# Moving the sum of two GRU cells from TensorE to VectorE for two column groups of a four-layer graph network

## The chip, the cores and the metric

The program runs on one core of one Trainium2 chip. The metric is device time of one execution in microseconds (us), taken as the median of several runs. The core has five engines that work at the same time, each through its own queue in order: TensorE (PE, matrix products into the accumulator memory PSUM), VectorE (DVE, element-wise work), ScalarE (ACT, activation functions and scaled copies), GpSimd (POOL) and SyncE (SP, which here starts transfers). They wait for each other through semaphores.

## The reference, cut to what matters

Four graph layers follow each other on 3327 nodes with 64 features. Each normalises the state, computes an update from the adjacency matrix and adds it to the state `X`. The change is in the third layer. It runs two GRU cells on the same hidden state `h` and adds both outputs, scaled row by row with the diagonal of the adjacency matrix:

```python
def gru_cell(x, h, w_ih, w_hh, b_ih, b_hh):
    gi = x @ w_ih.T + b_ih
    gh = h @ w_hh.T + b_hh
    ir, iz, inn = jnp.split(gi, 3, axis=1)
    hr, hz, hn = jnp.split(gh, 3, axis=1)
    r = jax.nn.sigmoid(ir + hr)
    z = jax.nn.sigmoid(iz + hz)
    n = jnp.tanh(inn + r * hn)
    return (1.0 - z) * n + z * h
...
    edge_output = gru_cell(node_support, h, w_ih_e, w_hh_e, b_ih_e, b_hh_e)
    edge_support = gat(h, A_node, A_edge, W_gat, a_gat)
    node_output = gru_cell(edge_support, h, w_ih_n, w_hh_n, b_ih_n, b_hh_n)
    return d_edge[:, None] * edge_output + d_node[:, None] * node_output
```

Both adjacency arguments are the same matrix, so both diagonals are the same. With the output of a cell written as n + z (h - n), the update of a node is its diagonal entry times four terms: z0 (h - n0) + n0 + z1 (h - n1) + n1, where 0 is the first (edge) cell and 1 the second (node) cell.

## The kernel before, in words

The 3327 nodes are padded to 26 tiles of 128. In this layer the data lie feature-major: a tile such as `hP` has 128 partitions (64 features of the first 13 node tiles, and 64 of the last 13) and 1664 columns (13 tiles of 128 nodes). The columns are worked in four groups, `COLS`: group 0 has four tiles (512 columns), groups 1, 2 and 3 have three each (384 columns). A step `u` is one cell on one group: steps 0 to 3 are the first cell on groups 0 to 3, steps 4 to 7 the second cell on groups 0 to 3.

Each step has these pieces, named as in the code:

- `products(u)` (lines 1968 to 1980): eight TensorE products into four PSUM banks. Two slots of two banks serve the even steps, two others the odd ones, so step u writes the banks of step u - 2.
- `sigmoids(u)` (line 1988): ScalarE makes the gates r and z. The buffer of z is used again three steps later.
- `before_tanh(u)` (lines 1995, 1996): VectorE makes the argument of the tanh from two PSUM banks and the gate r.
- `tanh(u)` (line 1999): ScalarE, in place, gives n. For the first cell n lies in `xh[0][0]` (the trace calls it xh), for the second in `deg`.
- `state(u)` (lines 2001 to 2015): VectorE makes o = z (h - n) with a subtraction (2008) and a product (2011). For the first cell o lies in `oP` (the trace calls it own), for the second in `hP` itself.

The queues are in program order. In turn u of the loop the order is `products(u)`, `sigmoids(u)`, `tanh(u - 1)`, then `before_tanh(u)`, copies for the second cell (`take2`, ScalarE), `state(u - 1)`. After the loop comes the way back to node-major layout:

- `turn_back(k)` (lines 2020 to 2032): for each 128-column block of group k, TensorE multiplies each term with the identity and adds the products up in PSUM, which transposes the block and sums its terms at once. A group with one term takes a plain transpose (2029). `turn_back(0)` and `turn_back(1)` write to one PSUM slot (banks 4 and 5), `turn_back(2)` and `turn_back(3)` to another (banks 6 and 7).
- `scale(k)` (lines 2038 to 2047): ScalarE multiplies with the diagonal, one 64-column piece per instruction; for group 3 VectorE does it in one (2042).
- `use(k)` (line 2051): VectorE adds to `X`.

The terms differ by group in the kernel before. In groups 0 and 1 TensorE sums four terms (own, xh, hP, deg). In group 2 VectorE adds xh to own (2013) and TensorE sums three. In group 3 VectorE sums all four (2013, 2010, 2015) and TensorE transposes one.

`turn_back(0)` stands in the last turn of the loop, after `tanh(6)` and ahead of `before_tanh(7)`. After the loop the order is: `tanh(7)`, `scale(0)`, `turn_back(1)`, `scale(1)`, `turn_back(2)`, `state(7)`, `use(0)`, `turn_back(3)`, `use(1)`, `scale(2)`, `scale(3)`, `use(2)`, `use(3)`. Waits are kept per slot, not per bank. So in the built program the first product of `turn_back(1)` waits for the last instruction of `scale(0)`, and `scale(2)` waits for the last transpose of `turn_back(3)`. The fourth layer begins on VectorE with the row sums of `X` (line 449), after the last `use`.

Of the kernel before, what the change touches and what calls it, by code (L numbers as in the profile page):

```python
# [49 lines left out]
def tile_gnn4(ctx: ExitStack, tc: tile.TileContext, x, adjT, att0, b0, w1, bias1, w_gat, a_gat,  # L50
# [1778 lines left out]
    def plain_gat(masks, zo, deg, first, wg, gru, H, parts, banks, last_x, finish, close):  # L1829
# [8 lines left out]
        C = len(COLS)  # L1838
        with ExitStack() as st:
            def bank(k):  # L1840
                return banks[k]

            def of(k, at=0):
                t, n = COLS[k]
                return slice(at + t * P, at + (t + n) * P)
# [39 lines left out]
            hP = pers.tile([P, HP], F32, name="hP")  # L1885

            xh = [[pers.tile([P, HP], F32, name=f"xh{g}{o}") for o in range(2)] for g in range(2)]
            oP = H.rearrange("p k o d -> p (k o d)")
# [3 lines left out]
            for _ in range(1):  # L1892
# [108 lines left out]
                def state(u):  # L2001


                    g, k = steps[u]
                    cs = of(k)
                    nn, z = nns[u], gates[u][1]
                    o, h = (oP, hP)[g][:, cs], hP[:, cs]
                    V.tensor_sub(o, h, nn)
                    if g == 1 and k == C - 1:
                        V.tensor_add(nn, nn, oP[:, cs])  # L2010
                    V.tensor_mul(o, o, z)
                    if g == 0 and k > 1:
                        V.tensor_add(o, o, nn)
                    if g == 1 and k == C - 1:
                        V.tensor_add(oP[:, cs], o, nn)
# [3 lines left out]

                def turn_back(k):  # L2020

                    terms = [oP] if k == C - 1 else [oP, hP, deg] if k > 1 else [oP, xh[0][0], hP, deg]
                    t0, n = COLS[k]
                    pt = turned[k] = bank(4 + k)
                    for t in range(n):
                        cs = slice((t0 + t) * P, (t0 + t + 1) * P)
                        for i, src in enumerate(terms):
                            if len(terms) == 1:
                                PE.transpose(pt[:, t * P:(t + 1) * P], src[:, cs], ident)
                            else:  # L2030
                                PE.matmul(pt[:, t * P:(t + 1) * P], src[:, cs], ident, start=i == 0,  # L2031
                                          stop=i == len(terms) - 1)
# [28 lines left out]
                for u in range(K):  # L2061
                    products(u)
                    sigmoids(u)
                    if u:
                        tanh(u - 1)
                    if u == K - 1:
                        turn_back(0)
                    before_tanh(u)
                    if u < C:
                        take2(u)  # L2070
                    if u:
                        state(u - 1)
                tanh(K - 1)
                scale(0)
                turn_back(1)
                scale(1)
                turn_back(2)
                state(K - 1)
                use(0)
                turn_back(3)  # L2080
# [108 lines left out]
```

## Time and profile before

| what | us |
|---|---|
| median of 3 runs (lowest, highest) | 721.95 (721.23, 726.72) |
| the profiled execution, whole | 726.15 |
| its span, first to last instruction | 724.4 |
| TensorE busy in the span | 639.9 (88%) |
| VectorE busy | 532.1 (73%) |
| ScalarE busy | 542.3 (75%) |
| first product of step 0 to last `use` | 430.39 to 465.74 |

The page of the profile gives busy time by engine, then the chain of work that ended last, followed back from the last instruction, with shares of the span. The timeline lists instructions by start and length in us, with the engine, the line of the kernel, output and inputs; a bracket at the end is the time that the engine was idle before and what released it. A product of two float32 operands shows as two TensorE instructions, so "x32" are 16 products. The table of stretches gives, for each, the busy time of the engines (with the number of instructions in brackets), and PEclk, the clock that TensorE was granted, as a share of full speed. All times count from the start of the span.

### The profile page before, as it was taken

Reading aid. Unit: us, or ns where it says so; the run is one execution under the profiler, and the core shown is the slowest. Engines: PE = TensorE matmul, PEld = TensorE weight load, DVE = VectorE, ACT = ScalarE, POOL = GpSimd, SP = SyncE. Lnnn points to the kernel's source line nnn. Section 1 sums busy time; section 2 is a strip of 40 time slices with the busy share of each in tenths; the row PEclk is TensorE's granted clock in tenths of the full one; section 3 lists DMA queues with packets and bytes.
Section 4 is the critical chain, followed back from the end, with each engine's and each line's share of the span. In section 5 each row is a group of like instructions: output and inputs, shape, how many; then the busy total and the mean of one; then the engine's idle time right before and its main releaser. Section 6 shows DMA issues by size and latency. Waiting matters only on the chain.

```text
span 724.4 us, 12112 instructions
## 1 busy us (share of the span) xinstructions
PE 639.9 (88%) x4291; PEld 262.8 (36%) x4291; DVE 532.1 (73%) x980; ACT 542.3 (75%) x720; POOL 433.4 (60%) x327
## 2 busy tenths in 40 slices
PE   0799999989999889989998999449999999999970
PEld 0522233333333333435445653442223433334320
DVE  6867778767777799999755429697767777777755
ACT  2778888878888785687881578368888889888853
POOL 2699999979999500305740000038887888888840
PEclk9999999999999999999999999869999999999995
DMA  3998888888888725489960000202234444443001
GB/s 64 315 288 262 267 267 261 277 254 260 282 252 274 254 81 199 140 292 328 404 243 1 2 1 1 94 18 76 91 94 135 118 119 139 117 118 117 24 2 51
DMA packets 61638, 119.25 MB, mean 165 GB/s; under 512 B 9568, under 2 KB 34048, under 8 KB 61568
## 3 DMA queue, kind: packets, MB, share of 16 engines
q1 hardware_dynamic: 57216, 118.38, 50.8%
q10 hardware_dynamic: 4352, 0.02, 0.3%
q8 instruction: 35, 0.57, 0.3%
q14 instruction: 35, 0.29, 0.1%
HBM read 115.64 MB, written 0.88 MB: 161 GB/s over the span
## 4 chain that ended last, share of the span: by engine, by line
PE 65%; DVE 13%; issue 6%; POOL 5%; DMA 4%; ACT 3%; SPq 2%; ACTq 1%; POOLq 0%; DVEq 0%
PE slot L653 18%; PE slot L661 10%; PE slot L632 9%; PE slot L633 8%; PE slot L1552 6%; PE slot L1859 5%; POOL sig L621 5%; PE slot L1566 4%; DMA adj<-in 3%; DVE same L1447 2%; PE slot L1975 2%; PE slot L2031 1%; DVE mask L1535 1%; ACT sig L618 1%; PE slot L1980 1%
## 5 line engine op out<-in xcount | busy, mean ns | idle before, releaser
L643 DVE SCALAR_TENSOR_TENSOR sig<-slot,sig 128x768 f32<-128x768 f32 (+2 forms) x209 | 212.8, 1018 | 112.9 <-POOL sig L621 108.0
L638 ACT ACTIVATE slot<-slot 128x768 f32<-128x768 f32 (+1 forms) x208 | 177.2, 852 | 59.6 <-PE slot L633 59.5
L621 POOL TENSOR_TENSOR sig<-adj,sig 128x768 f32<-128x768 f32 (+1 forms) x104 | 201.3, 1960 | 17.3 <-ACT sig L618 11.4
L618 ACT ACTIVATE sig<-leftB,right 128x768 f32<-128x768 f32 (+1 forms) x208 | 203.1, 976 | 0.1
L621 POOL TENSOR_TENSOR sig<-mask,sig 128x768 f32<-128x768 fp8e4 (+2 forms) x105 | 173.4, 1664 | 40.0 <-ACT sig L618 39.1
L653 PE MATMUL slot<-sig,Xr 128*64 128x384 f32 (+1 forms) x832 | 171.3, 530 | 7.0 <-DVE sig L643 6.9
L632 PE MATMUL slot<-XC,XT 128*128 128x384 f16 (+1 forms) x416 | 142.4, 342 | 2.6 <-ACT sum L671 1.7
L633 PE MATMUL slot<-XF,XE 73*128 73x384 f16 (+1 forms) x416 | 141.6, 340 | 0.0
L661 PE MATMUL slot<-sig,X 128*32 128x384 f32 (+1 forms) x832 | 95.7, 532 | 0.0
L1558 ACT ACTIVATE w<-slot,ebias 128x832 bf16<-128x832 f32 x76 | 69.1, 951 | 25.2 <-PE slot L1552 24.8
L653 PEld LDWEIGHTS slot<-sig,Xr 128*64 128x64 f32 x832 | 50.2, 136 | 88.4 <-issue 63.7
L632 PEld LDWEIGHTS <-XT 128*128 128x128 f16 x416 | 40.7, 98 | 95.3 <-issue 68.8
L1552 PE MATMUL slot<-mask,rest 128*128 128x416 fp8e4 x208 | 54.0, 341 | 5.2 <-ACT adj L1558 2.8
L1552 PE MATMUL slot<-mask,after 128*128 128x416 fp8e4 x208 | 53.4, 339 | 1.1 <-DVE deg L1576 1.1
L633 PEld LDWEIGHTS <-XE 73*128 73x128 f16 x416 | 40.8, 98 | 28.0 <-issue 3.6
L1447 DVE TENSOR_SCALAR_CACHE_REDUCE same<-late 128x832 fp8e4<-128x832 f32 x48 | 48.4, 1009 | 0.0
L219 POOL TENSOR_TENSOR mask<-mask,offdiag 128x128 fp8e4<-128x128 fp8e4 x26 | 17.5, 682 | 43.9 <-PE slot L1552 43.8
L436 POOL MEMSET X<- 128x832 f32 x2 | 1.6, 791 | 69.0 <-ACT xh L1966 69.0
L1859 PE MATMUL slot<-mask,own 128*64 128x384 fp8e4 (+1 forms) x416 | 39.8, 346 | 2.2 <-DVE deg L1576 2.2
L661 PEld LDWEIGHTS slot<-sig,X 128*32 128x32 f32 x832 | 16.5, 108 | 69.1 <-issue 66.7
L542 PE MATMUL pt<-ident_h,Xp 128*64 128x128 f16 x32 | 2.6, 314 | 37.6 <-ACT Xp L481 37.6
L1566 PE MATMUL slot<-w,h 128*64 128x416 bf16 x304 | 34.0, 345 | 0.0
(337 smaller groups left out, 699.4 us busy)
## 6 DMA issues: line engine op xcount, KB each, us to landing
adj<-in SPq DMA_DIRECT2D x78, 384.0 KB, 4.7
late<-in SPq DMA_DIRECT2D x48, 416.0 KB, 3.2
adj<-in SPq DMA_DIRECT2D x17, 832.0 KB, 7.2
adj<-in SPq DMA_DIRECT2D x27, 512.0 KB, 4.9
ahead<-in SPq DMA_DIRECT2D x14, 832.0 KB, 8.0
ahead<-in SPq DMA_DIRECT2D x16, 416.0 KB, 5.6
own<-in SPq DMA_DIRECT2D x16, 416.0 KB, 5.3
own<-in SPq DMA_DIRECT2D x8, 832.0 KB, 6.6
```

The source lines that it names most:

```text
L618: A.activation(sig, leftB[c], AF.Sigmoid, bias=right[:, b:b + 1])
L621: G.tensor_tensor(sig[:, os], adj[:, os], sig[:, os], op=OP.mult)
L632: PE.matmul(L[:, o, :c[1] * P], XT[:, rows], XC[c][:, o, :], start=True, stop=False)
L633: PE.matmul(L[:, o, :c[1] * P], XE[:KE, rows], XF[c][:, o, :], start=False, stop=True)
L638: A.activation(L, L, AF.Arctan, scale=PA / SX ** 2)
L643: V.scalar_tensor_tensor(sig[:, os], slot[:, os, :tiles[k][0][1] * P], PC, sig[:, os], op0=OP.add, op1=OP.mult)
L653: PE.matmul(acc[c][o * D:(o + 1) * D, 0, :n], Xr[:, b, :], sigs[k][:, o, :], start=b == 0, stop=b == T - 1)
L661: PE.matmul(acc[c][q:q + 32, 1, :n], X0[:, b - 1 + i, :], w[:, o, :], start=b == 1, stop=b == T - 1, tile_position=(0, q))
L1552: PE.matmul(cnt[o][:, h, :BK], w, cols(k, o, h), start=w is after and steps[k][1] == T - 1, stop=True, skip_group_check=True)
L1558: A.activation(ws[k][:, o, :, :], cnt[o][:, :, :BK], AF.Exp, scale=-LN2, bias=ebias)
L1566: PE.matmul(acc[c][o * D:(o + 1) * D, h, :BK], parts[i][:, b, :], w[:, o, h, :], start=b == T - 1 and i == 0, stop=b == 0 and i == 1)
L1859: PE.matmul(acc[k][o * D:(o + 1) * D, :], w, mask[:, of(k, o * HP)], start=n == 0 and i == 0, stop=n == T - 1 and i == 1)
```

## The change

VectorE adds n0 to own for every group of the first cell, not only for groups 2 and 3. For the second cell it adds own to `deg` in groups 0 and 1 as it did in group 3. TensorE then sums two terms in groups 0 and 1 (hP and deg), still three in group 2, and transposes one in group 3.

```diff
@@ state(u)
                     V.tensor_sub(o, h, nn)
-                    if g == 1 and k == C - 1:
+                    if g == 1 and k != 2:
                         V.tensor_add(nn, nn, oP[:, cs])
                     V.tensor_mul(o, o, z)
-                    if g == 0 and k > 1:
+                    if g == 0:
                         V.tensor_add(o, o, nn)
                     if g == 1 and k == C - 1:
                         V.tensor_add(oP[:, cs], o, nn)
@@ turn_back(k)
-                    terms = [oP] if k == C - 1 else [oP, hP, deg] if k > 1 else [oP, xh[0][0], hP, deg]
+                    terms = [oP] if k == C - 1 else [oP, hP, deg] if k == 2 else [hP, deg]
```

In the built program this takes 14 float32 products from TensorE's queue (8 in `turn_back(0)`, 6 in `turn_back(1)`) and puts four additions into VectorE's: line 2013 for steps 0 and 1, line 2010 for steps 4 and 5. Nothing else changes place on any engine, and no transfer is added or moved.

## The prediction

> **What bounds the kernel now.** First the page, then the chain of waits in order of time around the changed lines, then the timeline there, then the stretches with the granted clock. The page's shares say little here: the change touches 15 us of 724.
>
> ```profile
> span 724.4 us, 12112 instructions
> PE 65%; DVE 13%; issue 6%; POOL 5%; DMA 4%; ACT 3%; SPq 2%; ACTq 1%; POOLq 0%; DVEq 0%
> ```
>
> The chain at the end of the layer:
>
> ```profile
> 449.52 0.80 PE slot L1980 x8
> 450.32 3.78 PE slot L2031 x32
> 454.11 0.02 issue
> 454.13 1.75 ACT x L2047 x8
> 455.88 0.04 issue
> 455.93 6.58 PE slot L2031 x42
> 462.51 0.34 PE slot L2029 x3
> ...
> 462.88 1.34 ACT x L2047 x6
> ...
> 464.24 0.56 DVE x L2042
> ```
>
> TensorE leads through turn_back(0) (x32, 16 products), then scale(0) on ScalarE, then turn_back(1) and (2) (x42, 21 products) and the three transposes of turn_back(3). The removed products lie on this chain, 8 before scale(0) and 6 behind it. So the chain read alone promises a gain. Now VectorE and ScalarE beside it:
>
> ```profile
> 441.42 0.62 DVE L1995 SCALAR_TENSOR_TENSOR xh<-slot,gb,gate 128x384 f32<-128x384 f32 x1 [0.25 <-ACT gate L1988]
> ...
> 443.13 0.56 DVE L2011 TENSOR_TENSOR own<-own,gate 128x384 f32<-128x384 f32 x1
> ...
> 443.72 0.56 DVE L2013 TENSOR_TENSOR own<-own,xh 128x384 f32<-128x384 f32 x1
> ...
> 453.10 0.61 ACT L1999 ACTIVATE deg<-deg,gb 128x384 f32<-128x384 f32 x1 [1.56 <-DVE deg L1996]
> 454.13 1.75 ACT L2047 ACTIVATE x<-slot,dcol 128x64 f32<-128x64 f32 x8 [0.42 <-PE slot L2031]
> 454.63 0.56 DVE L2010 TENSOR_TENSOR deg<-deg,own 128x384 f32<-128x384 f32 x1
> 455.11 0.55 DVE L2011 TENSOR_TENSOR hP<-hP,gate 128x384 f32<-128x384 f32 x1
> ```
>
> tanh(7) waited 1.56 us for VectorE, and scale(0), next in ScalarE's queue, began only 0.42 us after tanh(7) had ended at 453.71. So VectorE is 0.42 us behind the lead, and from 441.42 on it has no idle row until 456.86.
>
> **The change, part by part.** The sum is made in the profiled execution's time (span 724.4, whole 726.15; the whole is 4.2 above the median of 721.95 and inside the runs' 721.23 to 726.72).
>
> *Added on VectorE ahead of tanh(7).* (a) own + xh on 512 columns, step 0: 0.72, the spacing of the equally wide steps before it (437.47 to 438.19). Its cover is small: before_tanh(2), next in the queue, could have started 0.60 after the product at 438.19, at 438.79, and started at 438.90, so 0.1 is absorbed. (b) The same on 384 columns, step 1: 0.59 (443.13 to 443.72), of which the 0.25 of idle before 441.42 absorbs as much. (c) deg + own, 384 columns, step 5: 0.48 (454.63 to 455.11; shorter because the product behind it doesn't need it). (d) The same on 512, step 4: 0.48 x 0.69/0.56 = 0.60. Together 2.39, less 0.35 absorbed: 2.0 us.
>
> Queued behind each are before_tanh of the next steps, and behind those tanh(7). It moves from 453.10 to 455.1. scale(0), which follows an independent ScalarE instruction by some 0.47 (1.05 for a pair of 0.58), starts at 455.55 where it was 454.13: 1.4 later (2.0 less the 0.42 and the overlap of 0.14). Its 1.75 is unchanged; turn_back(1) starts at 457.3 where it was 455.92.
>
> *turn_back(0).* It now starts with hP of step 4, ready at 449.76 before and (a), (b), (d) later, 1.55 together: 451.3. It needs 8 products x 0.2225 (15 spacings of the 16 old ones, 450.25 to 453.59) = 1.78: done at 453.1, one us sooner than before. This gains nothing, since scale(0) now waits for tanh(7) until 455.5; the 8 removed products are worth at most the 0.42. The products of step 7 write the banks that before_tanh(5) reads; that ends at 448.43 + 0.95 = 449.4, just as they want them (449.45): 0 to 0.1, hidden under the wait for hP. The gate z of step 7 waits for the buffer of step 4's product, now near 451.2; tanh(6) behind it needs before_tanh(6) at about 452.5 anyway. state(7)'s own is ready near 458.2 and turn_back(3) wants it after 462: 4 us of cover.
>
> *turn_back(1) and (2).* 15 products instead of 21, six fewer. At full clock six are 6 x 0.2225 = 1.34. That meets the 1.4 by which they start later: **net +0.05**.
>
> *The clock.* The 21 products took 455.92 to 462.24, 6.32 us, not 4.67:
>
> ```profile
> 450.47:453.88 3.41, 3.41 (x32) 3.41 (x31) 3.31 (x7) 1.44 (x3) 0.00 (x0) 1.00 0.00 0
> 453.88:457.30 3.42, 1.59 (x14) 1.40 (x14) 2.90 (x6) 1.75 (x8) 0.00 (x0) 1.00 0.00 0
> 457.30:460.71 3.41, 3.41 (x19) 3.41 (x18) 0.00 (x0) 0.48 (x3) 0.00 (x0) 0.50 0.00 0
> 460.71:464.12 3.41, 2.13 (x19) 1.89 (x18) 0.56 (x1) 2.10 (x11) 0.55 (x4) 1.00 0.19 33
> ```
>
> (First column TensorE's busy time, PEclk third from the end.) The clock was halved at 457.30 for 3.41 us, after a stretch of equal length in which TensorE was busy 1.59 of 3.42 (46%); 2.13 of 3.41 (62%) halved nothing at 464.12. A product costs 0.43 there (459.35 to 459.78), 0.21 more. Six at full, eight at half, seven at full clock: 1.34 + 3.44 + 1.56 = 6.34, as seen. With the change TensorE idles from 453.1 to 457.3 instead of 454.09 to 455.92. At the same places of the halving: 457.3 + 8 x 0.43 + 7 x 0.2225 = 462.3 against 462.24, again +0.05. But a program's start needn't fall alike. Bounds: the halving covers the products less than before, say 5 cold ones instead of 8: 0.05 - 3 x 0.21 = -0.6; or the old kernel met no halving and the new one 8 cold products: +1.7; or all 15 and the transposes cold: 15 x 0.21 + 0.35 = +3.5.
>
> The Trainium skill (TensorE: Matmul & The Clock Gate, "What's actually happening") says that TensorE falls to half rate after at least one idle window of about 3.4 us, and returns after a busy one. The row differs: a pause of 1.83 us was enough here, the window being half busy. By the page's rule the old pause would cost nothing and the new one of 4.2 would: 8 cold products, +1.7; the sum above goes by the rows.
>
> Take +0.05, the value at the places this trace shows: 721.95 + 0.05 = 722.0.
>
> **The rivals.** *VectorE has room (faster).* If the four additions cost the chain nothing, tanh(7) stays at 453.10, scale(0) gains its 0.42 and six products go: 0.42 + 1.34 = 1.8, or 0.42 + 6 x 0.43 = 3.0 with the six at half clock: 718.9 to 720.2. For it: TensorE's 65% of the chain. Against it: no idle VectorE row between 441.42 and 456.86. 10%.
>
> *The longer pause costs clock (slower).* TensorE's pause before turn_back(1) grows from 1.83 to 4.2 us. It decides where the old pause leaves its window more than about half busy and the new one doesn't: then 8 to 15 products run cold that ran at full clock, +1.7 to +3.5: 723.6 to 725.5. For it: 4.2 exceeds the 3.41 of a stretch, so some stretch before turn_back(1) is always nearly empty, while 1.83 needs a bad place. Against it: in this trace the old kernel paid already. 33%.
>
> *The change not done as said:* the built program has the 14 products fewer and the four additions, so no chance is left for it. Something unpriced, such as the halvings falling otherwise in the 220 us of products behind: 2%.
>
> **How the numbers follow.** The main case, net -0.6 to +1.0, has 55%; its time is 722.0. The range starts at 720.0, between the main case's lower bound on the lowest run (721.23 - 0.6 = 720.6) and the gain rival's 718.9 to 720.2, and ends at 727.0, the highest run before plus a little: the runs differ by 5.5 among themselves, more than any case, and a median can land up there. 1% is 7.2 us, about what a measurement of this kernel can tell from no change. No priced case reaches it in either direction, so within 1% gets 0.96, faster 0.015, slower 0.025. Inside 1% I lean to slower.
>
> **What would show it.** Right: tanh(7) near 455.1 relative to the same start (2.0 later against the first product of step 0); scale(0) released by tanh(7) and not by turn_back(0); a TensorE pause of about 4 us before turn_back(1); then 15 products in 3.3 us plus 0.21 for each cold one; last use within 1 us of 465.7. Wrong: VectorE idle rows between steps 2 and 7 that swallow the additions, scale(0) still released by TensorE, or the end of the layer moved by over 3 us.

## The result and the profile after

The changed kernel took 725.21 us (median of 20 runs, 720.72 to 730.72) against 722.3 (20 runs, 720.27 to 726.72): ratio 1.0039, interval 1.0021 to 1.0056, so 1.5 to 4.0 us slower. The time lies in the predicted range and within 1%, on the side it leaned to, but it is not the 722.0 of the likeliest case: it is what the rival "the longer pause costs clock" had priced at 723.6 to 725.5.

The profiled execution of the changed kernel doesn't show the loss. Its span is 722.2, 2.2 less than that of before. From the first ScalarE copy of step 0 to the first row sum of the fourth layer it takes 427.70 to 463.75 = 36.05 us, the old one 429.75 to 465.77 = 36.02. Its chain of waits in order of time (start, us, what):

```profile
451.84 0.54 DVE deg L1995
...
452.40 0.57 DVE deg L1996
...
452.99 0.61 ACT deg L1999
453.61 1.64 ACT x L2047 x8
...
455.29 5.20 PE slot L2031 x30
460.49 0.34 PE slot L2029 x3
...
460.85 1.34 ACT x L2047 x6
...
463.75 1.96 DVE mean L449 x2
```

The lead now comes from VectorE through tanh(7) into scale(0); turn_back(0) is no longer on it. The timeline of the same stretch:

```profile
452.99 0.61 ACT L1999 ACTIVATE deg<-deg,gb 128x384 f32<-128x384 f32 x1 [2.03 <-DVE deg L1996]
453.51 1.72 ACT L2047 ACTIVATE x<-slot,dcol 128x64 f32<-128x64 f32 x8
455.29 0.79 PE L2031 MATMUL slot<-ident,hP 128*128 128x128 f32 x2 [3.93 <-ACT x L2047]
```

scale(0) follows tanh(7) without the 0.42 us of idle it had. TensorE stands idle 3.93 us before turn_back(1), where it was 1.83. The stretches with the granted clock (TensorE's busy time first, PEclk third from the end):

```profile
448.40:451.81 3.41, 2.02 (x16) 1.86 (x16) 3.34 (x8) 1.20 (x2) 0.00 (x0) 1.00 0.00 0
451.81:455.22 3.41, 0.00 (x0) 0.00 (x0) 3.31 (x8) 2.23 (x9) 0.00 (x0) 1.00 0.00 0
455.22:458.64 3.42, 3.35 (x15) 3.35 (x16) 1.49 (x3) 0.40 (x3) 0.00 (x0) 0.50 0.00 0
```

A whole stretch of 3.41 us is empty, and the next is halved. In this pair of executions both kernels pay one halving, so the pair shows no difference. The other executions leave one number that tells of halvings, their mean granted clock. Call each stretch of 3.41 us at half clock a halving; the number of them per execution is (1 - clock) x 2 x span / 3.41. Over all 102 executions of the kernel before that went with the experiments it is 12.2 on average; over the 32 of the changed kernel 14.6 (14.8 in the first 20, 14.3 in the 12 below). In those 102 executions one halving more goes with 1.21 us more time (a straight line through them). 2.4 x 1.21 = 2.9 us, about the loss. This is a correlation over halvings at all places of the program; the last experiments below take many away that cost next to nothing.

### The profile page after: what moved, and what is told of

Read it like the earlier page. It is cut to its first block, busy times and chain, and to the rows that moved or that the text cites. A ratio compares the mean times of both kernels' runs of the same rounds, so it can differ in the third digit from the quotient of the medians.

```text
span 722.2 us, 12062 instructions
## 1 busy us (share of the span) xinstructions
PE 635.6 (88%) x4263; PEld 260.1 (36%) x4263; DVE 533.7 (74%) x984; ACT 542.4 (75%) x720; POOL 430.2 (60%) x327
## 4 chain that ended last, share of the span: by engine, by line
PE 69%; DVE 15%; issue 5%; POOL 5%; ACT 4%; ACTq 1%; DMA 1%; DVEq 0%; POOLq 0%
PE slot L653 20%; PE slot L661 11%; PE slot L632 10%; PE slot L633 9%; PE slot L1552 6%; PE slot L1859 5%; PE slot L1566 4%; POOL sig L621 4%; DVE same L1447 2%; PE slot L1975 2%; DVE mask L1535 1%; ACT sig L618 1%; DVE X L1605 1%; ACTq L322 1%; PE slot L1980 1%
## 5 line engine op out<-in xcount | busy, mean ns | idle before, releaser
L219 POOL TENSOR_TENSOR mask<-mask,offdiag 128x128 fp8e4<-128x128 fp8e4 x26 | 14.9, 583 | 47.1 <-PE slot L1552 47.1
```

## The experiments

Three theories. A: at equal clock both kernels are equally fast; the longer pause of TensorE brings more halvings. B: VectorE's additions cost more than the trace shows. C: the difference lies somewhere else in the program. "Path" below is the time from the first copy of step 0 to the first row sum of layer four in the one trace that each run leaves, "pause" TensorE's idle time before turn_back(1) there, "halvings" the mean over the run's 10 to 20 executions (for before over the 102), with the number that lies in the trace's path in brackets.

| kernel | path us | pause us | halvings (in the path) | ratio to before (interval) |
|---|---|---|---|---|
| before | 36.02 | 1.83 | 12.2 (1) | 1 |
| after | 36.05 | 3.93 | 14.8 (1) | 1.0039 (1.0021 to 1.0056) |
| c_before | 36.02 | 1.84 | 11.8 (1) | 1.0000 (0.9978 to 1.0022) |
| c_after | 36.10 | 3.93 | 14.3 (1) | 1.0037 (1.0016 to 1.0058) |
| fill_after | 34.45 | filled | 12.5 (0) | 1.0009 (0.9981 to 1.0037) |
| fill_before | 34.40 | filled | 12.0 (0) | 1.0010 (0.9991 to 1.0029) |
| only_g1 | 34.88 | 2.03 | 13.7 (1) | 1.0015 (0.9994 to 1.0037) |
| only_g0 | 37.52 | 3.46 | 13.1 (2) | 1.0030 (1.0006 to 1.0053) |
| removed_only | 35.39 | 3.08 | 14.0 (2) | 0.9995 (0.9971 to 1.0019) |
| adds_only | 37.18 | 2.53 | 12.8 (1) | 1.0027 (1.0000 to 1.0053) |
| g1_fill | 33.25 | filled | 12.7 (0) | 0.9983 (0.9969 to 0.9997) |
| after_edge | 36.11 | 3.94 | 9.0 (1) | 1.0016 (1.0003 to 1.0028) |
| before_edge | 34.41 | 1.84 | 7.6 (0) | 0.9998 (0.9982 to 1.0015) |
| g1_fill_edge | 33.25 | filled | 8.0 (0) | 0.9987 (0.9972 to 1.0001) |

### The two kernels again

No edit.

> The kernel before, unchanged, run as a kernel of its own, for the granted clock of each execution and a second trace. All theories: ratio 1.000 within its interval. Theory A (TensorE's clock at the end of the GRU layer): the executions differ by whole halvings of 3.41 us, and this kernel has fewer of them on average than the changed one (about one fewer). Theory B (VectorE's path is longer than the trace of after shows): the same number of halvings in both kernels. Theory C (the difference sits elsewhere in the program): the number differs, but the places are not at the end of the GRU layer.

> The changed kernel, unchanged, again. All theories: ratio near 1.004, 2 to 4 us slower. In the trace, from the first product of step 0 to the last use: 35.3 us as in both traces so far, plus up to 1.8 if more of the 15 products after scale(0) run at half clock (theory A).

Medians 722.05 and 725.11, the same distance again. The counts of halvings differ by 2.5 (11.8 and 14.3, standard error 0.5). Of the twelve executions of c_before six met about 11 and none more than 14; those of c_after run from 12 to 17. This speaks for A against B. In the trace of c_after the pause falls across two stretches; the emptier one is 21% busy, and the next, from 455.68 on, is halved:

```profile
452.27:455.68 3.41, 0.71 (x6) 0.71 (x7) 3.31 (x7) 2.25 (x9) 0.00 (x0) 1.00 0.00 0
```

### The pause filled

```diff
                     if u == K - 1:
                         turn_back(0)
+                        for _ in range(16):
+                            PE.matmul(bank(7)[:, :P], ident, ident, start=True, stop=True)
```

(7 in place of 16 in fill_before.)

> The changed kernel with 16 extra identity products (3.6 us at full clock) into a free bank behind turn_back(0), so that TensorE is busy in its pause before turn_back(1). The output is the same. Theory A: turn_back(1) to (3) run at full clock, the last use comes 1.7 us earlier than in the trace of after, and the time falls by 1.7 to 3.5 us against the changed kernel: 721.5 to 723.5, ratio 0.999 to 1.002. Theory B: no change against after, ratio 1.004. Theory C: the last use comes earlier in the trace, but the ratio stays above 1.002.

> The kernel before with 7 extra identity products (1.56 us) in its shorter pause of 1.83 us. The output is the same. Theory A: where the kernel before met a halving there (as in its trace) it meets none now, last use 1.7 us earlier than in its trace; on the median 0 to 1.0 us faster than before, ratio 0.998 to 1.000. Theories B and C: ratio 1.000.

The timeline of fill_after at the place, the extra products at line 2069:

```profile
450.35 3.74 PE L2069 MATMUL slot<-ident 128*128 128x128 f32 x32
454.44 0.49 PE L2031 MATMUL slot<-ident,hP 128*128 128x128 f32 x2 [0.35 <-ACT x L2047]
```

The pause is 0.35 us, and the stretch behind it keeps its clock:

```profile
455.40:458.81 3.41, 2.98 (x27) 2.75 (x26) 1.05 (x2) 1.73 (x8) 0.55 (x4) 1.00 0.00 0
```

The path falls from 36.05 to 34.45, by 1.6 (expected were 1.7 for eight cold products, that is, products at half clock). VectorE's additions are all still there, yet the time goes from 725.11 to 722.33 (means 2.06 apart, standard error 0.84) and 1.8 halvings of 14.3 go (standard error 0.7). B, which expected a ratio of 1.004, can't explain that. The ratio 1.0009 lies below the 1.002 of C as well, but its interval doesn't exclude C. fill_before reaches 34.40: at full clock too the two kernels are equal, within 0.05. It brought no measurable gain (1.0010, interval through 1; 0.1 halvings fewer than before, standard error 0.4). Since one halving in the path costs 1.6 us, this fits a kernel before that often met none here, although two of its three traces (before, c_before, before_edge) met one. How often it meets one stays open.

### One part alone

Group 1 alone, and group 0 alone with k == 0 in place of k == 1:

```diff
-                    if g == 1 and k == C - 1:
+                    if g == 1 and k in (1, C - 1):
                         V.tensor_add(nn, nn, oP[:, cs])
...
-                    if g == 0 and k > 1:
+                    if g == 0 and (k == 1 or k > 1):
...
-                    terms = [oP] if k == C - 1 else [oP, hP, deg] if k > 1 else [oP, xh[0][0], hP, deg]
+                    terms = [oP] if k == C - 1 else [hP, deg] if k == 1 else [oP, hP, deg] if k > 1 else [oP, xh[0][0], hP, deg]
```

> The change made for group 1 alone (384 columns): VectorE gets two additions (own + xh in step 1, deg + own in step 5), TensorE loses the 6 products of turn_back(1), turn_back(0) keeps its 16. The output is the same. By the sum's own rows (theory A's path): tanh(7) 0.8 later, turn_back(1) 0.15 to 0.3 later, six products fewer: 1.1 us shorter than before from the first ScalarE copy of step 0 to the first row sum of X (36.0 with one halving in it, so 34.9; 33.3 without). TensorE's pause stays at 1.8 to 2.4 us, so the halvings are those of before: 1 us faster than before, ratio 0.997 to 0.9995. If instead any addition on VectorE costs the whole program what the change cost (theory B): 1.002.

> The change made for group 0 alone (512 columns): two additions on VectorE (1.2 us, ahead of tanh(7)), the 8 products of turn_back(0) go, which lie before a start that now waits for tanh(7). The output is the same. Theory A: path 0.2 to 0.6 longer than before (36.2 to 36.6 with one halving), pause of TensorE about 4.0 us as in the changed kernel, so 1.5 to 2.5 more halvings per execution than before and 2 to 3 us slower: ratio 1.002 to 1.004. Theory B: half of the change's cost, 1.002.

Group 1's path is 34.88 where 34.9 was expected: its six products lie behind scale(0) and are saved in full, its two additions cost little. But the time missed the expectation: not 1 us faster, rather no different (1.0015, interval through 1), with 1.5 halvings more than before (standard error 0.6) where as many as before were expected. In its trace seven halved stretches in a row lie between the layers, where before has five. Group 0 is slower by what was expected (1.0030): its eight products lie before a start that waits for tanh(7), so only its additions and the longer pause count. But it has only 0.8 halvings more than before (standard error 0.5) where 1.5 to 2.5 were expected, and its pause is 3.46, not 4.0. Its stretches show what a halving that falls early in a pause does:

```profile
450.33:453.74 3.41, 0.91 (x9) 0.72 (x7) 3.31 (x7) 1.84 (x7) 0.00 (x0) 1.00 0.00 0
453.74:457.15 3.41, 2.45 (x11) 2.45 (x12) 2.35 (x5) 0.91 (x5) 0.00 (x0) 0.50 0.00 0
457.15:460.57 3.42, 3.42 (x18) 3.42 (x17) 0.00 (x0) 0.34 (x2) 0.00 (x0) 0.50 0.00 0
```

The halved stretch starts inside the pause, TensorE is busy for only 2.45 of its 3.41 us, and a second halved stretch follows: 13 to 14 cold products (5.87 us at 0.43) rather than 8, and a path of 37.52, about 1 us above the 36.2 to 36.6 expected with one halving.

### Only the products away, only the additions there

```diff
-                    terms = [oP] if k == C - 1 else [oP, hP, deg] if k > 1 else [oP, xh[0][0], hP, deg]
+                    terms = [oP] if k == C - 1 else [oP, hP, deg] if k == 2 else [hP, deg]
```

> The kernel before with the 14 products left out and no addition made: the output of groups 0 and 1 lacks n0 and own. Theory A: path 1.9 us shorter at equal clock (34.1 with one halving, 32.5 without), but a pause of 3.2 to 3.5 us, so 1 to 2.5 more halvings than before, which take back most of it: ratio 0.998 to 1.001. Theory B (only VectorE's additions cost): 1.9 to 3.0 us faster, ratio 0.996 to 0.9975, halvings as before.

The other keeps the terms and has, in `state`:

```diff
+                    if g == 1 and k < 2:
+                        V.tensor_add(wide_as(k, extra), nn, oP[:, cs])
...
+                    if g == 0 and k < 2:
+                        V.tensor_add(wide_as(k, extra), o, nn)
```

> The kernel before with the four additions at their places but into a tile that nothing reads; TensorE keeps all its products. The output is the same. Theory A: path 1.4 us longer (37.4 with one halving, 35.8 without), pause 2.4 us, at most one halving more than before: 1.4 to 2.5 us slower, ratio 1.002 to 1.0035. Theory B: the whole cost of the change and more, since the products stay: 4 us or more, ratio 1.0055.

With 14 products fewer and nothing added, the program isn't faster (0.9995, interval 0.9971 to 1.0019): the 1.9 us that its path saves at equal clock (turn_back(1) starts 0.54 sooner, and six products are 1.34) don't show in the time, and it has 1.7 more halvings (standard error 0.6). Under B it had to be at least 1.9 faster with as many halvings as before. The interval reaches to 2.1 us faster, so the time alone doesn't quite rule that out; the halvings speak against it. The additions alone cost 1.4 us in the mean (standard error 0.7), as A expected and less than B's 4 us, with a path of 37.18, 1.16 above before at one halving each; their pause is 2.53 and their halvings 12.8, hardly more than before.

### Between the layers

g1_fill has group 1's edit and eight products in the pause. The three others add the 70 products below to after (after_edge), to before (before_edge) and to g1_fill (g1_fill_edge):

```diff
                 turn_back(3)
+                for _ in range(70):
+                    PE.matmul(bank(0)[:, :P], ident, ident, start=True, stop=True)
                 use(1)
```

> Group 1's change alone plus 8 identity products in TensorE's pause before turn_back(1), to see whether the 1.1 us that group 1 saved on the path comes through once no halving follows. The output is the same. Theory A (the path plus halvings at the end of the layer, plus what their place does to the start of the next layer): path 33.3 us without halving, 11.5 to 12.5 halvings per execution, 1 to 2 us faster than before: ratio 0.997 to 0.999. If the products that group 1 lost were worth nothing: 1.000.

> The changed kernel with its pause before turn_back(1) left as it is, and 70 identity products (15.6 us at full clock) behind turn_back(3), so that TensorE doesn't stand idle between the layers. The output is the same. Theory A: the halving before turn_back(1) stays (path 36.05 or more), but no halving lies on the start of the fourth layer: first weighting of layer four (line 643) no later than 26.1 us after the first row sum, 0.5 to 1 sooner; 5 to 7 fewer halvings per execution than after; still about 1.3 slower than before_edge. If the whole cost of the change lay in the GRU layer: 2.3 slower than before_edge.

> The kernel before with the same 70 products behind turn_back(3). The output is the same. Theory A: 4 to 6 fewer halvings per execution than before, the start of layer four 0.5 to 1 sooner: ratio 0.998 to 1.000.

> Group 1's change, the 8 products in the pause and the 70 between the layers together. The output is the same. Theory A: path 33.3, no halving between the GRU layer and the middle of layer four, 2.5 to 3.5 us faster than before: ratio 0.995 to 0.9965.

g1_fill is faster than the kernel before, 721.77 against 722.88 (and than the changed one, at 725.1 to 725.2): ratio 0.9983 (0.9969 to 0.9997). What group 1 saves comes through once TensorE isn't idle before turn_back(1).

The edge kernels were made to see what the halvings do to the start of layer four. In c_after the clock came back one stretch later than in after, though TensorE was busy for 3.38 of the 3.42 us ahead:

```profile
479.57:482.99 3.42, 3.38 (x51) 3.17 (x50) 2.90 (x12) 2.58 (x6) 2.23 (x9) 0.50 0.03 7
482.99:486.40 3.41, 3.41 (x21) 3.41 (x20) 2.35 (x13) 0.59 (x1) 0.00 (x0) 0.50 0.41 87
```

In c_after the first weighting of layer four (line 643 on VectorE) starts at 490.82, 27.34 after the first row sum; in after 26.11, and the rest of the span is longer by as much (259.72 against 258.45). The same late return stands in the traces of only_g1 (27.85), removed_only (27.65) and g1_fill (27.52). g1_fill's pause is filled, so the late return doesn't need a halving there. All four are kernels with 15 products behind scale(0); after and fill_after, with 15 as well, don't show it, and none of the five with 21 does. But in these four traces a stretch began 16.1 to 16.8 us behind the first row sum, in the seven others without the 70 products 14.3 to 15.5, so it may be only where the stretches happened to fall. No run separates the two.

With the 70 products the first weighting starts 25.71 to 26.06 behind the row sum in all three edge kernels. That is at most 0.4 sooner than the 26.11 of before and after, where 0.5 to 1 was expected, and after_edge's trace still has a halving there (from 481.06 on). after_edge is still 1.9 us slower than before_edge (means, standard error 0.5), with 1.4 halvings more (standard error 0.45). Their traces put most of that in the GRU layer itself: paths of 36.11 and 34.41. Expected were 1.3 under A and 2.3 if all of it lay there; 1.9 doesn't tell them apart, so how much of the 2.8 us arises at the start of layer four stays open, and for that part C isn't excluded. before_edge itself gained nothing measurable from 4.6 fewer halvings: while VectorE normalises, a halved TensorE clock cost next to nothing. g1_fill_edge is no better than g1_fill: 1.2 us faster than before in the mean, where 2.5 to 3.5 were expected.

## Why the prediction was right and wrong

Times relative to the first copy of step 0, before and after:

- *The additions, 2.0 us ahead of tanh(7).* Right: 23.35 to 25.29, 1.94.
- *scale(0) 1.4 later, released by tanh(7).* Right: 24.38 to 25.81, 1.43; the 0.42 us idle is gone.
- *turn_back(0)'s eight products worth nothing.* Right: it is done 2.15 us before scale(0) starts.
- *turn_back(1) 1.4 later, six products saved, net +0.05.* Right at equal clock: 36.02 to 36.05 with one halving each, 34.40 to 34.45 with none.
- *The pause, 1.83 to 4.2 us.* 3.93.
- *"Take +0.05, the value at the places this trace shows".* This step failed. The one trace of before showed a halving in the pause, and the sum took it as the rule for both kernels; over all executions the changed kernel had 2.4 halvings more and was 2.8 us slower. c_before's trace has a halving at the place too, before_edge's none.
- *The rival "the longer pause costs clock".* It came true, but its argument that a pause of 4.2 always leaves some stretch nearly empty doesn't hold: the pause can fall across two stretches. What holds is weaker. A pause of 3.93 takes at least half of itself, 1.96 us, out of one stretch, which is then at most 43% busy; one of 1.83 can be split so that both stretches stay well over half busy, as in before_edge (77% and 69%). The price of 1.7 to 3.5 holds the measured 2.8, in part by luck: in each of the three traces of the changed kernel the pause cost one halving, 1.6 to 1.7 us, and the rest isn't accounted for; some of it may lie at the start of layer four. That the time lies in the range says little for the sum, since the upper end of 727.0 came from the scatter of the runs.
- *The page's rule.* The Trainium skill (TensorE: Matmul & The Clock Gate, "What's actually happening") asks for one idle window of about 3.4 us; by that rule the old kernel pays nothing, and the new one pays 1.7 where its pause covers a whole stretch. The traces differ: of the three with the changed kernel's pause of 3.93 only after's has an empty stretch, yet all three were halved (c_after behind a stretch 21% busy, after_edge behind one 36% busy), and so were two of three with the pause of 1.83.
- *The gain rival* fell with the additions' 1.94.
- Not foreseen: that halvings can also shift the start of layer four (26.1 to 27.3 and more), and that 15 products are a shorter burst than 21. In only_g1 and removed_only the stretch at the end of the layer was only 23% and 22% busy, and the halvings between the layers began 0.3 us ahead of the first row sum; in the other traces with such halvings they began 0.6 to 2.4 behind it. Both are shown in single traces; that they happen more often with the changed kernel is only inferred from the counts.

## What to carry to other kernels

When a change thins out TensorE's work between two waits, count the pause it opens as well as the products it saves: here 14 products fewer, with nothing added, gained nothing measurable, and group 1's six paid only with the pause filled. A profile shows one placing of the clock's stretches; where the granted clock moves in whole steps, compare the mean clock of many executions before taking one trace's stretch as typical. Move work only where both sides of the move lie on the path: group 1's products did, group 0's did not.

## What the runs showed of the hardware

- The clock is granted in stretches of 3.41 us whose place against the program differs from run to run: relative to the first row sum, an edge fell anywhere from 0.6 to 3.1 us behind it in the twelve traces that show a halving near it.
- A stretch that was 46% busy was followed by a halved one in the traces of before and c_before; so was one that was 53% busy (1.82 of 3.41, after_edge, 477.65 on); one that was 42% busy (1.45 of 3.42, c_after, 459.09 on) wasn't. A busy share as the profile counts it doesn't decide alone.
- At half clock, stretches 72% and 78% busy did not bring the clock back (only_g0, removed_only), nor did two 88% busy (only_g1, g1_fill). 91% and more mostly did, but 99% twice did not (c_after at 479.57, and the like in removed_only). The last four hold all or most of the 26 products of only six columns each (line 554).
- Identity products that nobody reads keep the clock up as others do: 16 of them took 1.8 halvings per execution away (standard error 0.7), 70 between the layers took away 4.6 from before.
